# A convolution kernel whose weight load is cut to nine taps and a bias, and whose weight copies are split between GpSimd and VectorE

## The chip, the cores and the metric

The kernel runs on one core of a Trainium2 chip. The metric is the time of one execution in microseconds, measured on the device. Lower is better. The time before is the median of three runs. A profile of one execution, taken by the hardware, goes with it; its span (82.0 us) is a little shorter than the measured time.

## The reference

The input `x` is a batch of 8 images with 32 channels of 128 x 128 numbers, float32. Each image is normalized in 16 groups of two channels, convolved with a 3x3 kernel (32 channels in, 32 out, written as a product of Fourier transforms of size 256), cut to size, and added to `x`:

```python
def _L0_conv_ref(x, weight, bias, stride, padding):
    ...                       # fft_H = fft_W = 256; fx, wf: transforms of x and weight
    fout = jnp.einsum('bihw,oihw->bohw', fx, wf)
    sp = jnp.fft.ifft2(fout, norm='ortho').real
    ...                       # out_h = out_w = 128
    sh = (fft_H - out_h) // 2
    sw = (fft_W - out_w) // 2
    out = sp[:, :, sh:sh + out_h, sw:sw + out_w]
    return out + bias[None, :, None, None]

def _gn(v, G=16, eps=1e-5):
    B_, C_, H_, W_ = v.shape
    g = v.reshape(B_, G, C_ // G, H_, W_)
    m = jnp.mean(g, axis=(2, 3, 4), keepdims=True)
    s = jnp.var(g, axis=(2, 3, 4), keepdims=True)
    return ((g - m) / jnp.sqrt(s + eps)).reshape(v.shape)

x = x + _L0_conv_ref(_gn(x), L0_conv_weight, L0_conv_bias, 1, 1)
```

The window that is cut out begins at row and column 64 of the transform. So only the upper left part of each output (66 x 66 of 128 x 128 numbers) holds a convolution; everywhere else the output is `x` plus the bias.

## The kernel before

The host splits each image into its even and odd rows and columns. The 128 partitions hold the four such quarters (`q = 0..3`) of 32 channels each, and an image is 64 x 64 numbers in each partition. A 3x3 convolution then becomes four products `k` (row shift `dr`, column shift `dc`), each with a 128x128 weight matrix that is filled with taps and zeros. The normalized part `g` of an image has 33 x 33 numbers in each partition.

A small layer (`put`) records every instruction with the tokens it needs, and turns them into semaphores. The five engines are called `pe` (TensorE), `dve` (VectorE), `act` (ScalarE), `pool` (GpSimd) and `sp` (SyncE). The instructions of each engine stand in the order in which they are put.

Loads first: image 0 in two halves, the weights by ScalarE's queue, then the other images, all of them into memory of their own.

```python
wb_sb = sbuf("wb_sb", *wb.shape)
...
for half in range(2):
    rows = slice(half * H // 2, (half + 1) * H // 2)
    loaded[0].append((rows.stop, load(xts[0][:, rows, :], x[0, :, 0, rows, :])))
    if half == 0:
        weights_in = load(wb_sb, wb, by="act")
for img in range(1, 4):
    loaded[img] = [(H, load(xts[img], x[img // 2, :, img % 2]))]
for pair in range(2, NPAIR):
    loaded[2 * pair] = loaded[2 * pair + 1] = [(H, load(pairs[pair], x[pair]))]
```

What comes before the first image's products. `pilot` takes a first guess of the mean, `sum_up` (VectorE) and `sum_squares` (ScalarE) take the sums of an image, `group` adds them over channels on TensorE, `keep_warm` is a matmul whose result nobody reads, and `take_std` makes the variance (VectorE), its root (ScalarE) and the scale.

```python
pilot(0); pilot_back(0); sum_up(0); sum_squares(0)      # one a line in the kernel
keep_warm(0, 2)
group(0, 0)

taps = wb_sb[:, 0 : 15 * C].rearrange("p (a b o) -> p a b o", a=5, b=3)
w5 = w_sb.rearrange("p (dr dc r k) -> p dr dc r k", dr=2, dc=2, r=2)
places = {
    0: ((0, slice(0, 1), slice(2, 3)), (1, slice(0, 2), slice(0, 2))),
    1: ((0, slice(0, 2), slice(1, 3)), (1, slice(1, 2), slice(0, 1))),
}
w_zero = put("pool", lambda e: e.memset(w_sb, 0.0), mark=True)
for q in range(4):
    rin, cin = q // 2, q % 2
    to = slice(q * C, (q + 1) * C)
    bias_ok = put("pool", lambda e: e.tensor_copy(bias_sb[to, :], wb_sb[:, 15 * C : 15 * C + 1]), weights_in, mark=True)
    for dc, c, b in places[cin]:
        w_ok = put("pool", lambda e: e.tensor_copy(
            w5[to, :, dc, :, c.start * C : c.stop * C],
            taps[:, 1 - rin : 5 - rin, b, :].rearrange("p (dr r) b o -> p dr r (b o)", dr=2),
        ), w_zero, weights_in, mark=True)
group(0, 1)
warm_ok = keep_warm(0, 1, w_ok)
pilot(1)
take_std(0)
normalize(0)
take_first(2, w_ok)
...
```

The loaded weights hold, for each of 32 input channels, five rows of three taps (rows 1, 2, a row of zeros, rows 0, 1 of the kernel), the bias, and 15 zeros: 496 numbers. The zero row lets one copy fill four rows at once.

Then the loop over images: `multiply` (four products for each of three chunks of 11 rows), `add` (VectorE adds product and bias to `x`), `add_bias` (GpSimd adds the bias to the rest), and a store for each pair of images or each image. After the last image three stores remain on SyncE's queue and one on GpSimd's. `add(img - 1, ...)`, the bias on GpSimd, and the matmuls of `keep_warm` are what `bias_ok` and `w_ok` are tokens for.

```python
for img in range(B):
    multiply(img, 0)
    multiply(img, 1, range(3))
    if img:
        add(img - 1, 0, NCHUNK)
        ...                                     # store the images that are finished
    group(img + 1)
    multiply(img, 1, range(3, 4))
    ...                                         # take_std, normalize, add_bias of the next
    multiply(img, 2)
    ...                                         # sums of image img + 2
...
stored = store(to[:, 0:N, :], xt[:, 0:N, :], biased[B - 1][1], *added[B - 1])
```

Of the kernel before, what the change touches and what calls it, by code (L numbers as in the profile page):

```python
# [153 lines left out]
def conv_preact_kernel(nc: bass.Bass, x: bass.AP, wb: bass.AP, out: bass.AP):  # L154
    NPAIR, _, _, H, W = x.shape
    B = 2 * NPAIR
    C = P // 4
# [7 lines left out]
    def sbuf(name, *shape):  # L165
        return nc.alloc_sbuf_tensor(name, list(shape), F32).ap()
# [4 lines left out]
    put = Queues(nc)  # L171

    pairs = [sbuf(f"x{pair}", P, 2, H, W) for pair in range(NPAIR)]
    xts = [pairs[img // 2][:, img % 2] for img in range(B)]


    wb_sb = sbuf("wb_sb", *wb.shape)
    loaded = {}

    def load(to, of, by="sp"):  # L180
        name = f"load{len(put.sems)}"
        put.semaphore(name)
        return put(by, lambda e: e.dma_start(to, of), adds=name)  # L183

    loaded[0] = []
# [5 lines that stand above are left out]
# [19 lines left out]
    bias_sb = sbuf("bias_sb", P, 1)  # L210
# [3 lines left out]
    for step, base in ((-1, 0), (1, 1)):  # L214
# [6 lines left out]
            pair_ok, mark=True,  # L221
# [12 lines left out]
        pair_ok, mark=True,  # L234
# [76 lines left out]
    def group(img, part=0):  # L311


        last = len(parts(img)) - 1
        of = to_sum(img, part)
        ok = put(
            "pe",
            lambda e: e.matmul(  # L318
                ps_ms[:, 0 : of.shape[1]], avg, of, start=(part == 0), stop=(part == last)
            ),  # L320
            *(sums_ok[img][part :: last + 1]), *([first_ok[img + 1]] if img and img + 1 < B else []),
            avg_ok, *means_read.get(img - 1, ()), mark=part == last,
        )
        if part == last:
            group_ok[img] = ok
# [117 lines left out]
    def keep_warm(first, times, *needs):  # L443
# [14 lines left out]

    taps = wb_sb[:, 0 : 15 * C].rearrange("p (a b o) -> p a b o", a=5, b=3)
    w5 = w_sb.rearrange("p (dr dc r k) -> p dr dc r k", dr=2, dc=2, r=2)
    places = {

# [4 lines that stand above are left out]
    for q in range(4):  # L469
        rin, cin = q // 2, q % 2  # L470
        to = slice(q * C, (q + 1) * C)
        bias_ok = put("pool", lambda e: e.tensor_copy(bias_sb[to, :], wb_sb[:, 15 * C : 15 * C + 1]), weights_in, mark=True)
        for dc, c, b in places[cin]:
            w_ok = put(
                "pool",
                lambda e: e.tensor_copy(  # L476
                    w5[to, :, dc, :, c.start * C : c.stop * C],
                    taps[:, 1 - rin : 5 - rin, b, :].rearrange("p (dr r) b o -> p dr r (b o)", dr=2),
                ),
                w_zero, weights_in, mark=True,  # L480
            )
    group(0, 1)
    warm_ok = keep_warm(0, 1, w_ok)
    pilot(1)
# [41 lines left out]
    xt, to = xts[B - 1], out[NPAIR - 1, :, 1]  # L526
# [67 lines left out]
```

## Time and profile before

| what | value |
|---|---|
| time, median of 3 runs | 83.28 us (83.2 to 83.3) |
| span of the profiled execution | 82.0 us |
| TensorE matmuls | 66.8 us busy, 222 matmuls |
| VectorE, ScalarE, GpSimd | 50.2, 47.9, 31.6 us busy |
| moved by DMA | 33.62 MB, 410 GB/s over the span |
| weight load | 62.0 KB, 3.6 us from issue to landing |

The profile is read in several views. The page gives the busy time of each engine, the busy share of engines and DMA in 40 slices of the span, the DMA queues, and groups of instructions. The chain of waits goes back from the last computing instruction to what released it, again and again. The timeline lists instructions with their start. The windows give the busy times in chosen stretches. In rows of a group or the timeline, `L476` is a line of the kernel, `w_sb<-wb_sb` are output and input, `32x128` is partitions by elements, and what stands in brackets is how long the engine stood idle before, and what ended that. A wait for several semaphores is put down to the one that came last by the profile, which isn't always the true one. "PE" is TensorE's multiplication, "PEld" its loading of weights, "SPq" SyncE's queue.

### The profile page before, as it was taken

Reading aid. Unit: us, or ns where it says so; the run is one execution under the profiler, and the core shown is the slowest. Engines: PE = TensorE matmul, PEld = TensorE weight load, DVE = VectorE, ACT = ScalarE, POOL = GpSimd, SP = SyncE. Lnnn points to the kernel's source line nnn. Section 1 sums busy time; section 2 is a strip of 40 time slices with the busy share of each in tenths; the row PEclk is TensorE's granted clock in tenths of the full one; section 3 lists DMA queues with packets and bytes.
Section 4 is the critical chain, followed back from the end, with each engine's and each line's share of the span. In section 5 each row is a group of like instructions: output and inputs, shape, how many; then the busy total and the mean of one; then the engine's idle time right before and its main releaser. Section 6 shows DMA issues by size and latency. Waiting matters only on the chain.

```text
span 82.0 us, 686 instructions
## 1 busy us (share of the span) xinstructions
PE 66.8 (81%) x222; PEld 41.3 (50%) x222; DVE 50.2 (61%) x43; ACT 47.9 (58%) x53; POOL 31.6 (39%) x43
## 2 busy tenths in 40 slices
PE   0009974999999999999999999999999999993000
PEld 0005433566666666666666656666666666660000
DVE  0009936960899499769949995996899324006000
ACT  3307967981699299569947974994798260000000
POOL 6876000004069900106992930490085029400000
PEclk9999998579999999999999999999999999999965
DMA  2899999999979979979959889989979999999995
GB/s 40 299 415 443 463 415 423 447 407 423 551 304 511 479 320 479 511 336 431 511 256 511 383 383 511 447 352 479 463 336 423 423 431 439 431 423 419 397 430 239
DMA packets 2164, 33.62 MB, mean 410 GB/s; under 512 B 296, under 2 KB 330, under 8 KB 500
## 3 DMA queue, kind: packets, MB, share of 16 engines
q1 hardware_dynamic: 2020, 33.36, 96.3%
q0 software_dynamic: 96, 0.19, 0.6%
q10 hardware_dynamic: 48, 0.06, 0.3%
HBM read 16.84 MB, written 16.78 MB: 410 GB/s over the span
## 4 chain that ended last, share of the span: by engine, by line
PE 74%; DMA 14%; DVE 2%; SPq 1%; issue 0%
PE ps L412 73%; DMA x<-x_dram 14%; DVE x L428 2%; PE ps_m L318 1%; SPq L183 1%; PE ps_w L265 0%
## 5 line engine op out<-in xcount | busy, mean ns | idle before, releaser
L412 PE MATMUL ps<-g,w_sb 128*128 128x363 f32 (+1 forms) x192 | 60.7, 473 | 0.1
L412 PEld LDWEIGHTS ps<-g,w_sb 128*128 128x128 f32 x192 | 36.1, 194 | 20.0 <-ACT origin L292 1.4
L283 DVE TENSOR_REDUCE sums<-x 128x1 f32<-128x4096 f32 x7 | 30.9, 4411 | 0.6 <-DMA x<-x_dram 0.6
L394 POOL TENSOR_SCALAR x<-x,bias_sb 128x1984 f32<-128x1984 f32 (+3 forms) x12 | 23.2, 1945 | 18.9 <-ACT origin L292 14.6
L303 ACT ACTIVATE unused<-x,origin 128x4096 f32<-128x4096 f32 (+1 forms) x9 | 30.0, 3330 | 0.3
L428 DVE SCALAR_TENSOR_TENSOR x<-ps,bias_sb,x 128x1089 f32<-128x1089 f32 (+2 forms) x9 | 10.9, 1220 | 7.7 <-PE ps L412 7.7
L373 ACT ACTIVATE g<-x,rstd 128x1089 f32<-128x1089 f32 (+2 forms) x8 | 9.4, 1190 | 3.4 <-DVE rstd L347 3.4
L283 DVE TENSOR_REDUCE first_sums<-x 128x1 f32<-128x2048 f32 x2 | 4.6, 2286 | 6.2 <-DMA x<-x_dram 6.2
L258 POOL COPY sums<-x 128x1 f32<-128x1 f32 x6 | 1.0, 186 | 18.2 <-DMA x<-x_dram 18.2
L335 DVE TENSOR_SCALAR var<-ps_m,square 128x1 f32<-128x1 f32 x8 | 1.8, 219 | 8.2 <-ACT square L330 8.2
L265 PE MATMUL ps_w<-x,avg 128*128 128x1 f32 x4 | 0.9, 304 | 7.1 <-POOL w_sb L476 6.1
L330 ACT ACTIVATE square<-ps_m,origin 128x1 f32<-128x1 f32 x8 | 2.1, 261 | 7.3 <-PE ps_m L318 7.3
L447 PE MATMUL ps<-x,avg 128*128 128x512 f32 x6 | 4.9, 942 | 0.0
L265 PEld LDWEIGHTS ps_w<-x,avg 128*128 128x128 f32 x4 | 0.8, 248 | 7.9 <-POOL w_sb L476 6.1
L318 PEld LDWEIGHTS ps_m<-sums,avg 128*128 128x128 f32 x16 | 2.8, 188 | 2.2 <-DVE x L428 1.0
L341 ACT ACTIVATE std<-var,eps 128x1 f32<-128x1 f32 x8 | 2.4, 294 | 2.3 <-DVE var L335 2.3
L344 DVE RECIPROCAL rstd<-std 128x1 f32<-128x1 f32 x8 | 1.3, 164 | 2.9 <-ACT std L341 2.9
L292 ACT ACTIVATE origin<-ps_w 128x1 f32<-128x1 f32 x2 | 0.3, 160 | 4.0 <-PE ps_w L265 4.0
L476 POOL COPY w_sb<-wb_sb 32x128 f32<-32x128 f32 (+1 forms) x8 | 2.5, 340 | 0.0
L318 PE MATMUL ps_m<-sums,avg 128*128 128x3 f32 x16 | 2.3, 214 | 0.0
L447 PEld LDWEIGHTS ps<-x,avg 128*128 128x128 f32 x6 | 1.5, 287 | 1.0 <-issue 1.0
L237 ACT ACT_TABLE_LOAD x1 | 1.3, 1283 | 1.2 <-PEq L579 1.2
(21 smaller groups left out, 13.3 us busy)
## 6 DMA issues: line engine op xcount, KB each, us to landing
x<-x_dram SPq DMA_DIRECT2D x2, 4096.0 KB, 34.3
out_dram<-x SPq DMA_DIRECT2D x2, 4096.0 KB
x<-x_dram SPq DMA_DIRECT2D x3, 2048.0 KB, 16.0
out_dram<-x SPq DMA_DIRECT2D x3, 2048.0 KB
x<-x_dram SPq DMA_DIRECT2D x2, 1024.0 KB, 6.2
out_dram<-x SPq DMA_DIRECT2D x1, 1056.0 KB
out_dram<-x SPq DMA_DIRECT2D x1, 800.0 KB
out_dram<-x POOLq DMA_DIRECT2D x1, 189.0 KB, 7.7
```

What stands on the lines that cost most here:

```text
L283: lambda e: e.tensor_reduce(to_sum(img, k)[:, 0:1], piece, mybir.AxisListType.X, ALU.add),
L303: lambda e: e.activation(unused[:, rows.start * W : rows.stop * W], piece, AF.Square, bias=origins[img], accum_out=to_sum(img, k)[:, 1:2],),
L318: lambda e: e.matmul(ps_ms[:, 0 : of.shape[1]], avg, of, start=(part == 0), stop=(part == last)),
L330: lambda e: e.activation(squares[img], ps_ms[:, 0:1], AF.Square, bias=origins[img]),
L335: lambda e: e.tensor_scalar(variances[img], ps_ms[:, 1:2], squares[img], None, op0=ALU.subtract),
L341: lambda e: e.activation(stds[img], variances[img], AF.Sqrt, bias=eps, scale=float(FFT * FFT)),
L373: lambda e: e.activation(g[:, rows, :], xt[:, LO + rows.start : LO + rows.stop, LO:W], AF.Identity, bias=rstd[:, 1:2], scale=rstd[:, 0:1],),
L394: put("pool", lambda e: e.tensor_scalar(part, part, 1.0, bias_sb, op0=ALU.mult, op1=ALU.add), *free, mark=mark)
L412: lambda e, k=k, dc=dc, rows=rows, top=top: e.matmul(ps[:, 0:rows, 0 : N - dc], w_sb[:, k * P : (k + 1) * P], g[:, top : top + rows, dc:N] ...
L428: lambda e: e.scalar_tensor_tensor(part, in0=ps, scalar=bias_sb, in1=part, op0=ALU.add, op1=ALU.add),
L447: "pe", lambda e: e.matmul(pss[1][:, 0, :], avg, piece, start=True, stop=True),
L476: lambda e: e.tensor_copy(w5[to, :, dc, :, c.start * C : c.stop * C], taps[:, 1 - rin : 5 - rin, b, :].rearrange("p (dr r) b o -> p dr r ( ...
```

## The change

Only the nine taps and the bias are loaded: 289 numbers for each input channel in place of 496, so 37 KB in place of 62. The zero row, the doubled row and the padding are gone. As the taps no longer lie so that one copy can fill four rows, each of the former eight copies becomes two, and GpSimd makes sixteen. The four copies of the bias move from GpSimd to VectorE. It is meant to load fewer bytes, and to take the bias off GpSimd. The set of places that are filled is the same; where a zero was copied before, the clearing of `w_sb` provides it.

```diff
-    taps = wb_sb[:, 0 : 15 * C].rearrange("p (a b o) -> p a b o", a=5, b=3)
+    taps = wb_sb[:, 0 : 9 * C].rearrange("p (a b o) -> p a b o", a=3, b=3)
     w5 = w_sb.rearrange("p (dr dc r k) -> p dr dc r k", dr=2, dc=2, r=2)
 ...
     for q in range(4):
         rin, cin = q // 2, q % 2
         to = slice(q * C, (q + 1) * C)
-        bias_ok = put("pool", lambda e: e.tensor_copy(bias_sb[to, :], wb_sb[:, 15 * C : 15 * C + 1]), weights_in, mark=True)
+        bias_ok = put("dve", lambda e: e.tensor_copy(bias_sb[to, :], wb_sb[:, 9 * C : 9 * C + 1]), weights_in, mark=True)
         for dc, c, b in places[cin]:
-            w_ok = put(
-                "pool",
-                lambda e: e.tensor_copy(
-                    w5[to, :, dc, :, c.start * C : c.stop * C],
-                    taps[:, 1 - rin : 5 - rin, b, :].rearrange("p (dr r) b o -> p dr r (b o)", dr=2),
-                ),
-                w_zero, weights_in, mark=True,
-            )
+            for dr, r, a in places[rin]:
+                w_ok = put(
+                    "pool",
+                    lambda e: e.tensor_copy(
+                        w5[to, dr, dc, r, c.start * C : c.stop * C],
+                        taps[:, a, b, :].rearrange("p a b o -> p a (b o)"),
+                    ),
+                    w_zero, weights_in, mark=True,
+                )
 ...
         "wb_dram": np.concatenate(
-            [
-                np.insert(weight.transpose(1, 2, 3, 0)[:, [1, 2, 0, 1]], 2, 0, axis=1).reshape(C, 15 * C),
-                np.asarray(L0_conv_bias).reshape(C, 1),
-                np.zeros((C, 15), x.dtype),
-            ],
-            axis=1,
+            [weight.transpose(1, 2, 3, 0).reshape(C, 9 * C), np.asarray(L0_conv_bias).reshape(C, 1)], axis=1
         ),
```

## The prediction

> **What bounds the kernel now.** I read the page's first parts, then the chain of waits in order of time, then the last ten microseconds, and last the timeline of the start. From the page, the TensorE row, the DMA shares in 40 slices, and the queues:
>
> ```profile
> PE 66.8 (81%) x222; PEld 41.3 (50%) x222; DVE 50.2 (61%) x43; ACT 47.9 (58%) x53; POOL 31.6 (39%) x43
> ...
> DMA  2899999999979979979959889989979999999995
> ...
> q1 hardware_dynamic: 2020, 33.36, 96.3%
> q0 software_dynamic: 96, 0.19, 0.6%
> q10 hardware_dynamic: 48, 0.06, 0.3%
> ```
>
> Two things run without a pause: TensorE (81% of the span) and the sixteen DMA engines (full in nearly every slice, the queue of x and out alone 96.3%). Queue q10 holds the weight load. The chain that ended last names TensorE:
>
> ```profile
> 1.73 11.62 DMA x<-x_dram
> 13.34 0.04 issue
> 13.39 0.38 PE ps_w L265 x2
> 13.77 0.07 issue
> 13.84 6.14 PE ps L412 x14
> ...
> 71.55 3.01 PE ps L412 x10
> 74.56 0.02 issue
> 74.58 1.48 DVE x L428 x2
> ```
>
> It begins with x arriving until 13.34 us (image 1, for which the second pilot product waits), then runs from one matmul to the next until the last addition ends at 76.06. But the span is 82.0, and what fills the last 6 us is seen in the windows (columns: stretch, length, busy time of PE, PEld, DVE, ACT, POOL, clock, DMA share, GB/s):
>
> ```profile
> 30.00:70.00 40.00, 40.00 (x142) 25.21 (x141) 31.11 (x27) 28.68 (x31) 18.14 (x14) 1.00 0.99 421
> 70.00:74.00 4.00, 4.00 (x16) 2.64 (x15) 0.00 (x0) 0.00 (x0) 0.72 (x2) 1.00 1.01 430
> 74.00:76.00 2.00, 0.55 (x3) 0.04 (x1) 1.42 (x2) 0.00 (x0) 0.00 (x0) 1.00 0.97 412
> 76.00:78.00 2.00, 0.00 (x0) 0.00 (x0) 0.06 (x1) 0.00 (x0) 0.00 (x0) 1.00 0.95 393
> 78.00:80.00 2.00, 0.00 (x0) 0.00 (x0) 0.00 (x0) 0.00 (x0) 0.00 (x0) 0.67 1.02 428
> 80.00:82.00 2.00, 0.00 (x0) 0.00 (x0) 0.00 (x0) 0.00 (x0) 0.00 (x0) 0.50 0.57 241
> ```
>
> The last store is issued at 76.1 us and holds 1056 KB (1.08 MB). From 76.1 to the end the DMA part of the trace counts 2.08 MB. So 1.00 MB of older stores still stood in the queue then, at 0.421 MB per us about 2.4 us of work. The end is therefore set by the whole volume, 33.62 MB, passing through DMA engines that are full; the multiplications have something like 2.4 us to spare. That is my choice against the chain, which stops at the last computing instruction.
>
> [...] the groups of this trace, kept apart by shape, have 394 ns for a copy of 256 elements and 286 for 128, so 0.84 ns[...]. [...] Here the reduction that ran beside the copies took 2.29 us, and the one after them 2.29 as well: no contention to be seen, and none to be added.
>
> **The change part by part.** These are the rows of the start, from the timeline (start, duration, engine, work):
>
> ```profile
> 4.46 0.18 POOL L472 COPY bias_sb<-wb_sb 32x1 f32<-32x1 f32 x1 [0.46 <-DMA wb_sb<-wb_dram]
> 4.59 0.62 POOL L476 COPY w_sb<-wb_sb 32x128 f32<-32x128 f32 x2
> ...
> 7.00 0.63 POOL L476 COPY w_sb<-wb_sb 32x256 f32<-32x256 f32 x2
> ...
> 11.28 1.10 PE L447 MATMUL ps<-x,avg 128*128 128x512 f32 x2
> 11.45 0.26 ACT L330 ACTIVATE square<-ps_m,origin 128x1 f32<-128x1 f32 x1 [0.47 <-PE ps_m L318]
> 11.75 0.22 DVE L335 TENSOR_SCALAR var<-ps_m,square 128x1 f32<-128x1 f32 x1 [0.99 <-ACT square L330]
> ```
>
> (1) The load. Removed: 32 x (1984 - 1156) = 26,496 B. At 421 GB/s that is 0.063 us of the full stream. Worked the other way: between 2 and 5 us the 48 packets of q10 took 7.6% of the engines' time, so 0.076 x 3 = 0.23 us of all sixteen; if this shrinks with the bytes (1156/1984 = 0.58), 0.10 us go. Of the stream I take 0.06 to 0.10 us off. A full stream hands that on to the end, whatever happens in between.
>
> (2) GpSimd. Before, four bias copies of 180 ns, four copies of 286 and four of 394: 3.44 us by durations, but 3.17 by the clock (4.46 to 7.63), because neighbours overlap by some 25 ns. After, sixteen copies: per quarter one of 32 elements, two of 64 and one of 128. From 180 ns for one element and 0.84 ns for each more: 206, 233 twice, and 286 (measured) make 958 ns a quarter, 3.83 us for four, less 15 overlaps of 25 ns: 3.46 us. So the weights are complete at about 7.9 us instead of 7.63, 0.3 us later. Who waits for that? Only the last warming matmul, which stands on TensorE behind the statistics of image 0 and began near 11.3. Over 3 us are to spare. (The trace puts the first pilot's wait at 6.10 down to these copies; that is a label, as the pilot began before the copies were done, and x had landed just then.) This costs nothing.
>
> (3) VectorE. Four copies of the bias, 32x1. They stand behind the second reduction of image 0, which ends at 10.76, and in front of the variance at 11.75, before which VectorE sat idle for 0.99 us, waiting for ScalarE's square (11.45 + 0.26). Small VectorE operations in this trace take 164 (reciprocal) to 219 ns; even four times 219 is 0.88 us, which just fits; with 164 they end at 11.42. Nothing is delayed. They leave GpSimd, where they were 0.7 us; that saving is inside step 2.
>
> (4) Addresses: everything behind the weight buffer moves down by 800 B[...]; I expect no effect. The zero row of the taps isn't copied any more; the clearing of the weights already wrote those zeros, and it stays.
>
> Sum: -0.06 to -0.10 us from (1), 0 from (2), (3), (4). From 83.28 that is **83.2 us**.
>
> **The rivals.** *TensorE is the bound after all*, as the chain has it. Then the end follows the first multiplication, at 13.84. Its start hangs on image 1's landing at 13.34, which stands behind the weight load in the same DMA engines, and so moves 0.06 to 0.10 us earlier too; the first part of g must be ready as well, which began at 12.78. Against this theory speaks the 2.4 us of older stores. It would give 83.2 as well, so the time alone won't separate the two. *The copies become the wait*: the sixteen would have to last until 11.3, that is 6.8 us, or 0.43 us each, where the trace has 0.39 for eight times the size of the smallest. Even then the backlog of 2.4 us should hide it: 83.3. If both the copies were slow and the backlog an illusion, 1 us late would be 84.3. *VectorE's copies delay the variance*: if they took 0.3 us each, 1.2 in all, the variance would come 0.2 us late, and g with it; the pilot product ended at 13.77 and hid most of that: 83.3. *Ragged rows are slow*: [...] should each of the 32 need 0.25 us more than now, [...] that is 32 x 0.25 / 16 = 0.5 us more for the stream: 83.7. This is the rival that I can least exclude, since the rows of x, which make up nearly all that is loaded, begin and end on round addresses.
>
> **Range and chances.** The three runs before lie within 0.1 us. The parts that I know add up to less than 0.1 us; the ones I don't, mainly the ragged rows, reach some tenths upward, and run to run and chip to chip another 0.1 or 0.2 either way. So 82.95 to 83.55. Two per cent would be 1.67 us: more than the whole weight load costs, which excludes faster; slower would need two rivals at once. Chances 0.02, 0.96, 0.02.
>
> **What would show it.** Step 1: q10 with about 0.04 MB and a smaller share of the stretch 2 to 5 us; if its time doesn't fall with the bytes, the ragged rows cost something. Step 2: sixteen copies of some 200 to 290 ns, ending near 7.9, and the warming matmul still near 11.3. Step 3: four small copies between 10.7 and 11.5 on VectorE, the variance still near 11.7. The bound: DMA shares still full to 80 us, first multiplication within 0.1 us of 13.84. I should be wrong if the weights landed much later than 4.4 us, if x came late, or if the span moved by over 0.3 us.

## The result, and the profile after

| | before | after |
|---|---|---|
| time, median | 83.22 us (83.17 to 83.30, 6 runs) | 83.88 us (83.59 to 84.29, 6 runs) |
| ratio, with 95% interval | | 1.0079 (1.0051 to 1.0107) |
| span of the profiled execution | 82.03 us | 82.05 us |
| time of that execution | 83.26 us | 83.97 us |
| time less span | 1.23 us | 1.92 us |

The changed kernel is 0.66 us slower. The last two rows already say where to look: the span, which is all that the page of a profile describes, is 0.02 us longer. Nearly all of the loss lies outside it.

First the inside. These are the DMA queues on the page of after:

```profile
q1 hardware_dynamic: 2020, 33.36, 96.6%
q0 software_dynamic: 96, 0.19, 0.6%
q10 hardware_dynamic: 48, 0.04, 0.1%
```

The weight load has shrunk to 0.04 MB. The timeline of the start, by start, duration, engine and work:

```profile
4.25 3.33 POOL L476 COPY w_sb<-wb_sb 32x32 f32<-32x32 f32 x16 [0.25 <-DMA wb_sb<-wb_dram]
...
10.46 0.66 DVE L471 COPY bias_sb<-wb_sb 32x1 f32<-32x1 f32 x4
...
11.06 1.10 PE L446 MATMUL ps<-x,avg 128*128 128x512 f32 x2
11.24 0.26 ACT L329 ACTIVATE square<-ps_m,origin 128x1 f32<-128x1 f32 x1 [0.47 <-PE ps_m L317]
11.53 0.22 DVE L334 TENSOR_SCALAR var<-ps_m,square 128x1 f32<-128x1 f32 x1 [0.41 <-ACT square L329]
```

All sixteen weight copies stand on GpSimd (POOL), so only the bias has moved to VectorE, whatever the title may suggest. They take 3.33 us and end at 7.58, the four bias copies take 0.66 us in the gap of VectorE, and the variance, which waits for ScalarE's square as before, comes at 11.53 (11.75 before). In the groups of GpSimd that are kept apart by shape, the copies are these:

```profile
L476 POOL COPY w_sb<-wb_sb 32x64 f32<-32x64 f32 x8 | 1.7, 229 | 0.1
L476 POOL COPY w_sb<-wb_sb 32x128 f32<-32x128 f32 x4 | 1.1, 286 | 0.1
L476 POOL COPY w_sb<-wb_sb 32x32 f32<-32x32 f32 x4 | 0.8, 202 | 0.3 <-DMA wb_sb<-wb_dram 0.3
```

The chain of waits, in order of time, stands 0.2 us earlier than the one shown before from the landing of x on, and the windows of the end show the DMA engines full to 80 us again:

```profile
1.73 11.40 DMA x<-x_dram
...
13.63 6.14 PE ps L411 x14
...
74.35 0.03 issue
74.38 1.48 DVE x L427 x2
```

```profile
74.00:76.00 2.00, 0.34 (x2) 0.00 (x0) 1.48 (x2) 0.00 (x0) 0.00 (x0) 1.00 1.03 437
76.00:78.00 2.00, 0.00 (x0) 0.00 (x0) 0.00 (x0) 0.00 (x0) 0.00 (x0) 1.00 0.94 391
78.00:80.00 2.00, 0.00 (x0) 0.00 (x0) 0.00 (x0) 0.00 (x0) 0.00 (x0) 0.62 1.03 434
80.00:82.00 2.00, 0.00 (x0) 0.00 (x0) 0.00 (x0) 0.00 (x0) 0.00 (x0) 0.50 0.62 262
```

The last data packet ends at 81.64 us; before, at 81.62. A first multiplication that came 0.2 us earlier (13.63 against 13.84) bought nothing at the end: when the last store was issued, at 75.88, 2.21 MB were still to pass, 1.13 MB more than that store holds (1.00 before).

Now the outside. The DMA view of a trace can be asked for the stretch behind the span, here 82 to 86 us. Before, it is empty; after, there are two packets, in a queue that the page doesn't list, as it has no packet within the span:

```profile
DMA packets 0, 0.00 MB, mean 0 GB/s; under 512 B 0, under 2 KB 0, under 8 KB 0
```

```profile
DMA packets 2, 0.02 MB, mean 4 GB/s; under 512 B 0, under 2 KB 0, under 8 KB 0
## 3 DMA queue, kind: packets, MB, share of 16 engines
q14 instruction: 2, 0.02, 1.5%
```

The kind of queue 14 is `instruction`, and these two packets hold 8192 B each; one of them is called a fetch below. The packets of that size in the two traces, in ns from the span's start:

```
before: -10535 -10502  -8281  -7815  -7765  -7735
after:  -10600 -10586  -8357  -8170  -7880  -7743   83771  83812
```

Six of them come ahead of the kernel in both, from -10.6 to -7.7 us. After has two more, and they come 2.1 us behind the last data packet (81.64). The last nine signals of the trace, all of one semaphore, show a gap there too: 83141 to 83180 before, 83161 to 83391 after, so one of them is about 0.2 us late. But it comes some 0.4 us ahead of the two packets, and two of the runs below (e5, e12) have the loss without such a delay, so it can't be most of the price. What differs in length is the program of two engines: GpSimd's has 62 instructions (57 before: four copies more, and one more that waits), VectorE's 49 (45).

### The profile page after: what moved, and what is told of

It reads as the page before. It is cut to its first block, busy times and chain, and to the rows that moved or that the text cites. A ratio compares the mean times of both kernels' runs of the same rounds, so it can differ in the third digit from the quotient of the medians.

```text
span 82.0 us, 695 instructions
## 1 busy us (share of the span) xinstructions
PE 66.8 (81%) x222; PEld 41.4 (50%) x222; DVE 50.7 (62%) x47; ACT 47.9 (58%) x53; POOL 31.8 (39%) x47
## 4 chain that ended last, share of the span: by engine, by line
PE 74%; DMA 14%; DVE 2%; SPq 1%; issue 0%
PE ps L411 73%; DMA x<-x_dram 14%; DVE x L427 2%; PE ps_m L317 1%; SPq L182 1%; PE ps_w L264 0%
## 5 line engine op out<-in xcount | busy, mean ns | idle before, releaser
L476 POOL COPY w_sb<-wb_sb 32x64 f32<-32x64 f32 (+2 forms) x16 | 3.2, 236 | 0.4 <-DMA wb_sb<-wb_dram 0.3
```

The source lines that it names most:

```text
L476: lambda e: e.tensor_copy(w5[to, dr, dc, r, c.start * C : c.stop * C], taps[:, a, b, :].rearrange("p a b o -> p a (b o)"),),
```

## The experiments

Three theories. G: GpSimd's longer program makes it fetch a further block of instructions after the last store. V: the same, or something else, on VectorE. R: the ragged rows of the load. In what follows, the number of an engine's instructions is that of the built kernel, waits included, and "time less span" is taken from the profiled execution where nothing else is said. Each experiment was timed beside runs of the kernel before, whose medians were 83.30 to 83.36 us; a ratio refers to those.

**e1: bias on VectorE alone.** The kernel before with

```diff
-        bias_ok = put("pool", lambda e: e.tensor_copy(bias_sb[to, :], ...), weights_in, mark=True)
+        bias_ok = put("dve", lambda e: e.tensor_copy(bias_sb[to, :], ...), weights_in, mark=True)
```

> The kernel before, with its 62 KB load and eight copies, but the four bias copies on VectorE: GpSimd's program has 54 instructions (57 before, 62 after), VectorE's 49 (45 before, 49 after). Theory G (GpSimd's longer program makes it fetch two more blocks of instructions after the last store, and that lengthens the end): 83.2 us, and no instruction fetch after the span. Theory V (it is VectorE's longer program, or the bias there): 83.9, with the fetch. Theory R (the ragged rows of the load, or what they displace): 83.2.

Measured: 83.39 us, ratio 1.0004 (0.9987 to 1.0021), no fetch after the span, time less span 1.23. V falls: VectorE has its 49 instructions and its bias copies here.

**e2: five idle memsets on GpSimd.** The kernel before with

```diff
+    spare = sbuf("spare", P, 8)
...
     take_first(2, w_ok)
+    for n in range(5):
+        put("pool", lambda e: e.memset(spare[:, n : n + 1], 0.0))
```

> The kernel before with five GpSimd memsets of one number per partition more, on a buffer that nobody reads, at about 18.5 us where GpSimd has nothing to do: 62 instructions, as after; load and VectorE as before. Theory G: 83.9 us, span 82.0, two instruction fetches of 8192 B after the span. Theories V and R: 83.2 and none.

Measured: 84.00 us, ratio 1.0070 (1.0054 to 1.0086), time less span 1.83. The whole loss of the change comes back with nothing of the change but five instructions that do nothing. The stretch from 82 to 86 us of this run:

```profile
q14 instruction: 2, 0.02, 1.3%
q1 hardware_dynamic: 1, 0.00, 0.0%
```

(The span was 82.6 here, so one data packet falls into the stretch.)

**e3: the load back to 62 KB.** The kernel after with

```diff
-            [weight..., np.asarray(L0_conv_bias).reshape(C, 1)], axis=1
+            [weight..., np.asarray(L0_conv_bias).reshape(C, 1), np.zeros((C, 207), x.dtype)], axis=1
```

> The kernel after, its rows padded to 496 numbers again, so that 62 KB are loaded in rows of 1984 B: GpSimd 62 and VectorE 49 instructions. Theory G: 83.9 with the fetch. Theory V: 83.9. Theory R: 83.2. Should the smaller load bring anything by itself, this is slower than after by 0.06 to 0.2 us.

Measured: 83.99 us, ratio 1.0066 (1.0048 to 1.0084), two fetches after the span, time less span 1.93. R falls: rows of 1984 B with the long program are as slow as after. Nor is the run slower than after by more than its interval, so the 25 KB are not seen.

**e4: the 37 KB load with a short GpSimd program.** The kernel after, with the block of weight copies put ahead of `pilot(0)` and its last five copies on ScalarE (`ON_POOL` is 11):

```diff
-                w_ok = put("pool", lambda e: e.tensor_copy(...), w_zero, weights_in, mark=True)
+                by = "act" if done >= ON_POOL else "pool"
+                done += 1
+                w_ok[by] = put(by, lambda e: (e.copy if by == "act" else e.tensor_copy)(...), w_zero, weights_in, mark=True)
```

> The kernel after with its 37 KB load, five of the sixteen copies on ScalarE and all of them put before the first image's statistics; GpSimd is back at 57 instructions, VectorE at 49, ScalarE at 54. Theory G: 83.0 to 83.2 us, without the fetch. Theory V: 83.9. Theory R: 83.9.

Measured: 83.43 us, ratio 1.0006 (0.9988 to 1.0025), time less span 1.23, nothing fetched after the span. The change's load and its sixteen copies without the loss. The 83.0 at the lower end of the expectation wasn't reached. One fetch shows inside the span, at 68.9 us.

**e5, e6, e7: two, four, thirteen memsets.** As e2 with another number in `range`, and 32 numbers for each partition in `spare`.

> The kernel before with two more GpSimd memsets instead of five: 59 instructions there. Theory G says that it is a step at some count between 57 and 62, from about 83.3 to about 84.0 us, with the fetch after the span or without it, and nothing between. The rival, call it S, that each further GpSimd instruction costs its share (0.66 us by five): 0.13 each, so 83.6 us.

> Four more: 61 instructions. Theory G: either 83.3 without the fetch or 84.0 with it. Rival S: 83.85.

> Thirteen more: 70 instructions. Theory G: 84.0 us, as with five, with the same two fetches. Rival S: 13 x 0.13 = 1.7 us more than before, 85.0.

Measured: two, 84.21 us, 1.0096 (1.0078 to 1.0114), one fetch after the span; four, 83.75 us, 1.0063 (1.0039 to 1.0087), but no fetch in the profile, and in all four executions a time less span of 1.25 to 1.32, so that what made them slow lies inside their spans of 82.2 to 82.7 us; thirteen, 83.44 us, 1.0008 (0.9986 to 1.0030). Rival S, a price for each instruction, falls with the last: eight instructions more than e2 and 0.56 us faster. But G's "84.0 as with five" fell as well. With thirteen the fetch is inside the span, at 71.5 us, while the stores run; in the stretch from 71 to 72 us it is one packet among those of the stores:

```profile
q1 hardware_dynamic: 40, 0.39, 93.3%
q14 instruction: 1, 0.01, 1.9%
...
out_dram<-x POOLq DMA_DIRECT2D x1, 189.0 KB, 7.7
```

The last line says that GpSimd issued its own store in this very stretch, so that store and the fetch fall in the same microsecond. So theory G takes a new form: what costs is neither the number of instructions (70 here, at 1.0008) nor a fetch as such (this one at 71.5 us), but a fetch that falls behind the last store (83.8 us in after, 84.4 in e2, at 1.0079 and 1.0070).

**e8: seventeen memsets on VectorE.** As e2, but `put("dve", ...)`, seventeen of them, ahead of `pilot(0)`.

> The kernel before with 17 small VectorE memsets between 0.8 and 5.8 us, where VectorE waits for x anyway: VectorE's program has 62 instructions, GpSimd's 57. If the step belongs to any engine whose program grows to GpSimd's length, 84.0 us with fetches after the span; if VectorE's program has a different length outside the kernel's own instructions, 83.3 and none.

Measured: 83.75 us in only four runs, 1.0053 (1.0035 to 1.0071); one fetch at 79.3 us, within the span, and time less span 1.23. So VectorE's end is as in before; what makes this run slow is inside its span of 82.7 us (its last data packet ended at 82.2), and the reason for it stays open.

**e9: after, with eight idle memsets more.** The edit of e2 on the kernel after, with `range(8)`.

> The kernel after, unchanged but for eight idle GpSimd memsets more at about 18.5 us: GpSimd's program has 70 instructions, as in the run with thirteen memsets, whose fetch fell at 71.5 us and cost nothing. Theory G, in its new form (what costs is a fetch of instructions that falls behind the last store; a still longer program makes the engine pass that place earlier, where it is hidden): the fetch moves into the span, time less span falls from 1.9 to about 1.25, and the time from 84.0 to 83.3 us, although work was added. Rival S (each instruction costs): 85 us. Rival R (the load): 84.0, as after.

Measured: 83.38 us, 1.0014 (1.0004 to 1.0024) over 22 runs, where after itself was at 1.0079. Time less span is 1.24. This run adds work to the changed kernel and takes some 0.5 us off it. The timeline of GpSimd shows the added work, 0.34 us of it:

```profile
18.68 0.34 POOL L490 MEMSET spare<- 128x1 f32 x8
```

In its trace the fetch lies at 71.5 us, as in e7, and behind 82 us only the rest of the data is left (the span was 82.7 here):

```profile
DMA packets 2, 0.01 MB, mean 2 GB/s; under 512 B 1, under 2 KB 1, under 8 KB 1
## 3 DMA queue, kind: packets, MB, share of 16 engines
q1 hardware_dynamic: 2, 0.01, 0.5%
```

**e10, e11, e12: four again, three, one.** As e2.

> The kernel with four more memsets (61 instructions) once more, since its profile showed no fetch and 1.29 between time and span, but its other times were up to 83.95. Theory G with a fetch that falls behind the end in most executions only: median 83.7 to 84.0 again, and a profile that may show the fetch, then with 1.8 to 1.9 between time and span. If 61 is truly free of it: 83.3 to 83.4.

> Three more: 60 instructions. Theory G: 84.0 us with the fetch after the span, as with 59 and 62. If the counts that pay alternate: 83.3.

> One more: 58 instructions, the shortest program that is longer than before. Theory G: a step must lie between 57 (83.3) and 59 (84.2), so either of the two, nothing between; time less span 1.25 or 1.85.

Measured: four again, 83.45 us, 1.0028 (1.0011 to 1.0045), no fetch again, 1.30; three, 83.98 us, 1.0084 (1.0067 to 1.0100), fetch, 1.91; one, 83.97 us, 1.0083 (1.0068 to 1.0097), fetch, 1.69. The kernel before with a single idle instruction more loses as much as with the whole change (1.0083 and 1.0079). And 61 is an exception in the middle of the costly lengths, twice: none of its fifteen executions has a time less span above 1.32.

**e13, e14: two instructions more on another engine.** As e8 with two; and two `e.activation(spare..., eps, AF.Sqrt)` on ScalarE behind the first one.

> The kernel before with two idle VectorE memsets more (47 there, GpSimd stays at 57). If it is GpSimd's own length: 83.3 us, no fetch after the span. If it is the layout of the whole program, which two instructions shift just as well: 84.0 with the fetch.

> The kernel before with two small ScalarE instructions more at about 2.8 us, where ScalarE is idle (50 there, GpSimd 57). GpSimd's own length: 83.3, no fetch after the span. Layout: 84.0.

Measured: VectorE, 83.42 us, 1.0008 (0.9988 to 1.0029), no fetch, 1.23. ScalarE, 83.56 us, 1.0026 (1.0009 to 1.0043), and a fetch after the span, at 83.57, with 1.47. So not every small shift of the program does it (e13); but two instructions more on ScalarE went with a late fetch too, and with 0.24 us more outside the span than before (1.47 less 1.23). The 0.24 us aren't there each time: three of the twenty executions have a time less span of 1.21 to 1.27, the others 1.37 to 1.58. Neither branch of what was expected for e14 describes that.

**e15, e16: seven and nine on GpSimd.** As e2.

> The kernel before with seven idle GpSimd memsets more: 64 instructions. If the range that pays reaches from 58 to nearly 70: 84.0 us, time less span 1.85. If it has ended: 83.3 to 83.5, and a fetch inside the span.

> Nine more: 66 instructions. As with seven: 84.0 if the range still holds, 83.3 to 83.5 and a fetch inside the span if it has ended.

Measured: seven, 83.74 us, 1.0019 (0.9998 to 1.0040), two fetches after the span, 1.73 (this ratio can't be told from 1; the late end is read from the time less span, 1.43 to 1.80 in all six executions); nine, 83.34 us, 0.9994 (0.9980 to 1.0007), one fetch at 81.4, just inside the span of 82.0, and 1.24. The range ends between 64 and 66. In the last microsecond of e16, 81 to 82 us, the fetch runs beside the last stores:

```profile
q1 hardware_dynamic: 22, 0.08, 18.7%
q14 instruction: 1, 0.01, 1.9%
```

All runs by GpSimd's instructions; the others differ from before or after in what their paragraphs say:

| GpSimd | run | last fetch, us | time less span, us | median, us |
|---|---|---|---|---|
| 54 | e1 | before the start | 1.23 | 83.39 |
| 57 | before | before the start | 1.23 | 83.22 |
| 57 | e13 | before the start | 1.23 | 83.42 |
| 57 | e14, ScalarE 50 | 83.6 | 1.47 | 83.56 |
| 57 | e4, ScalarE 54 | 68.9 | 1.23 | 83.43 |
| 57 | e8, VectorE 62 | 79.3 | 1.23 | 83.75 |
| 58 | e12 | 83.8 | 1.69 | 83.97 |
| 59 | e5 | 84.7 | 1.82 | 84.21 |
| 60 | e11 | 83.8 | 1.91 | 83.98 |
| 61 | e6, e10 | before the start | 1.29, 1.30 | 83.75, 83.45 |
| 62 | after | 83.8 | 1.92 | 83.88 |
| 62 | e2 | 84.4 | 1.83 | 84.00 |
| 62 | e3 | 84.0 | 1.93 | 83.99 |
| 64 | e15 | 83.8 | 1.73 | 83.74 |
| 66 | e16 | 81.4 | 1.24 | 83.34 |
| 70 | e7 | 71.5 | 1.24 | 83.44 |
| 70 | e9 | 71.5 | 1.24 | 83.38 |

The rule of the table has no exception: a last fetch that is in the span or ahead of it goes with 1.23 to 1.30 us outside the span, one that comes after it with 1.47 to 1.93. The executions that weren't profiled agree. Their spans are on record to 0.1 us: the runs of the table with no fetch behind the span have 1.19 to 1.32 us outside it in all 119 executions, the kernel before 1.18 to 1.30 in 162, and those with a late fetch, e14 aside, 1.38 to 2.01 in 65. So the two groups don't overlap.

The size of the loss follows the fetch as well. In after the last packet ends at 84.30 us from the span's start (83.81 and 0.48), and the measured time is 83.97: 0.33 less. In e14, with the smallest loss, the two are 83.88 and 83.56: 0.32 less. In all eight profiled executions with a late fetch this difference is 0.32 or 0.33 us, while the time outside the span goes from 1.47 to 1.93. The measured time moves with the end of the last packet, and the closing signals don't explain it: in after the last of them stands at 83.68, ahead of both packets.

A program far shorter than that of before was not tried; e1, with three instructions less, has the same 1.23 us outside the span.

## Why the prediction was wrong, point by point

**The load** was right in kind and worth nothing in the end. Between 2 and 5 us, q10 took 3.8% of the engines' time (7.6% before), 0.11 us less, against 0.06 to 0.10 predicted. But the runs with 62 KB and the same start show 5.8% (e1) and 5.9% (e3), so a fair share of that was the one profile of before; against them it is 0.06 us, as predicted. That a full stream hands such a saving on to its end was my estimate; a gain at the end of the run is not seen: e4 with 37 KB stands at 1.0006 (0.9988 to 1.0025), e16 with 62 KB at 0.9994 (0.9980 to 1.0007). The predicted 0.1% is inside these intervals and can't be told from nothing. The ragged rows, the rival that I could least exclude, show no loss in e4, and at most 0.2 us in e9 (1.0014, 1.0004 to 1.0024), which has eight idle instructions more as well.

**GpSimd's copies** were right in every time: 202, 229 and 286 ns (206, 233, 286 predicted), 3.33 us in all (3.46), no one waiting for them. The step that failed is this one all the same, in its last sentence: "This costs nothing." The prediction counted what sixteen copies take and who waits for them, and not that they make the program five instructions longer, when one more (e12) already went with a fetch behind the last store, at 83.8 us. That term, 0 in the sum, measured 0.69 us in the profiled pair (1.92 - 1.23), and e2 and e12 show it with the copies left as before. None of the signs that the prediction listed could have shown it, since all of them lie inside the span.

**VectorE's copies**: 131 to 147 ns each, 0.66 us in all, ended at 11.1, variance not delayed. Right, and e1 shows it alone. The range of 164 to 219 ns that the prediction read for small VectorE operations left out a copy of 145 ns in the same trace, which was the closest model.

**The bound**: right for the span, as far as these runs go. The last data packet ended at 81.62 and 81.64 us although the multiplications began 0.2 us apart. In e12 the last store was issued 0.9 us earlier than in before (75.19 against 76.09), and the data still ended at 81.73; this speaks against the rival that TensorE is the bound. The first multiplication, at 13.63, missed the 0.1 us around 13.84 that were forecast, but e1 and e3 with 62 KB have it at 13.68 and 13.65, so it wasn't the smaller load that moved it. What I took for granted was that the end of the span is the end of the time. I had 83.28 and 82.0 side by side and never asked what the 1.3 us between them are made of.

**The range**: 82.95 to 83.55 left room upward for slow DMA rows only, a cause inside the span; 83.88 lies above it. The 0.1 or 0.2 us for runs and chips fit the medians of the kernel before beside the experiments, 83.30 to 83.36 us on four chips, but not its single runs, which reached from 83.14 to 84.14. The chances were right in that the change stayed within 2%.

**What stays open.** Why 61 instructions escape while 60 and 62 pay. What waits for the fetch: the measured time moves with its end, but the trace has the packets and not the waiter, and that anything waits at all is not shown. That it is GpSimd's fetch is inferred from the lengths of the programs. And what in e8's span took 0.4 us.

## What to carry to other kernels

When a kernel is slower and its span isn't, compare time less span, and ask the DMA view for what lies behind the span. In this kernel one idle instruction more on GpSimd (e12) went with a fetch at 83.8 us, behind the last store, and with 1.69 us outside the span against 1.23; eight more on the changed kernel (e9) went with a fetch at 71.5 us, and with 1.24 against 1.92. So a small change is tested against the same kernel with a few idle instructions more or fewer; if those move the time as much as the change does, the change's own work is not what was measured.

## What was not expected of the hardware

The packets of 8192 B on the queue of kind `instruction` take 307 to 619 ns each in these traces (324 to 568 in before and after); six of them stand ahead of the kernel in before and after (four to seven in all). With one or two of them after the last store, the profiled executions have 0.24 to 0.70 us more outside the span (1.47 to 1.93 less 1.23). One inside the span went with ratios of 0.9994 to 1.0014 (e4, e7, e9, e16); in the stretch around it the stores' queue had a share of 93.3 to 105.6% in e4, e7 and e9, and of 18.7% in e16. Only e8, with 1.0053, is unexplained. A longer program was faster here: 62 instructions on GpSimd took 83.88 us, and the same kernel with eight idle ones more 83.38 (ratios of 1.0079 and 1.0014).
